# A routed mixture-of-experts kernel: one lookup of slots moved behind the first turned slots, the row copies issued from GpSimd, two counts put into one PSUM bank

## The chip, the cores and the metric

The kernel runs on one core of a Trainium2 chip. A core has a matrix engine (TensorE, "PE" in the profile, with its weight loads "PEld"), a vector engine (VectorE, "DVE"), a scalar engine (ScalarE, "ACT"), GpSimd ("POOL") and SyncE ("SP"), each with its own in-order instruction queue. They share an on-chip memory of 128 partitions (SBUF) and a small accumulator memory (PSUM) in eight banks, which TensorE writes and DVE and ACT read. DMA transfers are issued from the queues of SP, ACT and GpSimd. The metric is the device time of one execution in microseconds (us).

## The reference, cut to what matters

```python
xn  = layernorm(x)                                   # 8192 tokens of 512
out = x + attn(xn) + ffn(xn)

def attn(x):                                         # random features
    feats   = AB/sqrt(512) * exp(x @ (ab*G).T - 0.5*|x|^2*ab^2)
    return feats @ weights.T                         # weights: the same map of a 512x512 matrix

def ffn(x):                                          # 64 experts, 8 per token, at most 256 slots each
    scores = sigmoid(x @ router_w)
    # keep the 4 best of 8 groups of experts, then the 8 best experts
    w      = topk / sum(topk) * 2.5
    pos    = how many earlier (token, choice) pairs went to the same expert
    # the first 256 tokens of each expert fill its slots
    y[e]   = (silu(slots[e] @ gate[e]) * (slots[e] @ up[e])) @ down[e]
    return scatter_add(y * w) + shared_expert(x)
```

## The kernel before

Every product that must be exact is made from a high and a low part (`products`: three matmuls of high·high, high·low and low·high for each 128-row piece); `upper` (ACT, line 98) makes the high part and `rest` (DVE, line 101) the low one.

**Routing stage.** The 8192 tokens are 16 blocks of 512. `dense(b)` runs for the even blocks only and yields ten times: two steps of the shared expert (`ps_gu`), four of the random features (`ps_f`), four of the outputs (`ps_o`, first the shared expert's down product, then the attention). After each step `routing` moves the front of up to two blocks on, so that one pair of blocks passes in ten steps. A block's front is the generator `look_up`: it turns the block's rows (`ps_x`, line 331), forms the logits (`ps_l`, 364), turns them back (`ps_lt`, 381), ranks groups and experts on DVE (397 to 438), and two steps later counts: `ps_b` (443) gives for each expert the tokens in earlier chunks, `ps_u` (454) the running count within chunks, which ACT copies to `cu` (462) and SP stores to DRAM as `upto`. In the step after that DVE adds `ps_b` up in `begun` (482, two rows). By then the next block's front has started. In the first five steps of a pair (ps_gu, ps_f) the counts belong to an even block and the turning to an odd one; in the last five (ps_f, ps_o) the other way round.

**The rows of a block.** `statistics` (275, 278) and `roots` (DVE 241, 242, then thirteen small steps on GpSimd, 246 to 290, and four more for the norms to 294) feed `normalize`, in which ACT writes the normed rows to `xw` (301), two tiles of two 128-row groups. From block 5 on, `xc` (314) is a plain DMA copy of `xw`, 512 KB a tile, that TensorE may read as float32r, in which it turns the rows faster; it is issued from ACT's queue.

**PSUM.** Three pools: `ps_tr` (two banks), `ps_mm` (four), `ps_sm` (two, tag "sm"). `ps_l`, `ps_lt`, `ps_b`, `ps_u`, half of the `ps_x` tiles, and later `ps_fu` and `ps_y` of the late blocks' attention take the two "sm" banks in turn. A tile gets a bank once its last user has read it.

**Hand-over to the experts.** `seek` (the generator `slots`) finds which token fills which slot. Each step issues two lookups `at` from GpSimd (`find`, 699); once four experts are there, `tokens_of` (711 to 720) counts on DVE and gives `who`, the indices of the gathers `xg` (752, GpSimd). Eight steps run at the end of the last dense block, then gathers for experts 0 to 3. Then the last four steps of a late block's attention (`ps_y`; DVE copies each to `yb`, 594) take two more steps of `slots`, the second of which holds `tokens_of` for experts 4 to 7. Its DVE rows are kept behind what `last["dve"]` names. `turn_slots(0)` turns the first expert's gathered rows (`ps_t`, 769), splits them into `gT`, and computes their weights `shares` and `we` (779, 783).

**Experts' stage.** For each expert: `hidden` (`ps_gu` in 256 columns), `turn_slots` of the next, pieces of the late blocks' attention, `down` (`ps_e`), and a scatter-add of the rows from GpSimd (819). Weights come by SP.

**Order.** A scheduler fixes each engine's order when the program is built. `behind(a, b)` forces a behind b without a wait; `in_turn` keeps GpSimd's lookups, gathers and scatters in program order. Waits are semaphores that the framework places.

Of the kernel before, what the change touches and what calls it, by code (L numbers as in the profile page):

```python
# [9 lines left out]
FP = mybir.dt.float32  # L10
# [8 lines left out]
P = 128  # L19
T = 8192  # L20
H = 512
R = 512
E = 64
# [8 lines left out]
TB = 512  # L32
NB = T // TB
NS = TB // P
# [19 lines left out]
def rfs_attention_moe_kernel(  # L54
# [15 lines left out]
    nc = tc.nc  # L70
# [6 lines left out]
    ps_sm = ctx.enter_context(tc.tile_pool(name="ps_sm", bufs=2, space=PSUM))  # L77
# [6 lines left out]
    def kib4(shape, name, dt=FPR):  # L84
        return four.tile(shape, dt, tag="four", name=name)
# [11 lines left out]
    def upper(dst, src):  # L97
        return nc.scalar.copy(dst, src)  # L98

    def rest(dst, src, hi, on=nc.vector):  # L100
        return on.tensor_tensor(dst, src, hi.bitcast(FP), ALU.subtract)  # L101
# [15 lines left out]
    def behind(a, b):  # L117

        tc.add_manual_dep(a.ins, b.ins.name, ORDER, reason="what a needs comes late")
# [38 lines left out]
    def store_rows(b, k, xb):  # L158

        r0 = b * TB + k * UT  # L160
        return nc.sync.dma_start(
            out[r0 : r0 + UT, :].rearrange("(s p) d -> p s d", p=P), xb.t[k]
        )

    last = {}
# [131 lines left out]
    def normalize(b, rstd, shift):  # L297
        xb = xbs[b]
        xw = [rows.tile([P, NH, XW], FP, tag="xw", name="xw") for _ in range(NS // NH)]
        for s in range(NS):  # L300
            normed_s = nc.scalar.activation(
                xw[s // NH][:, s % NH, :H],
                xb[s],
                AF.Identity,
                bias=shift[:, s : s + 1],
                scale=rstd[:, s : s + 1],
            )
            behind(normed_s, last["upper"])
        xc = None
        if b >= ROUND:  # L310

            xc = [kib4([P, NH, H], "xc", FP) for _ in xw]
            for t, w in zip(xc, xw):
                nc.scalar.dma_start(t, w[:, :, :H])
        if b % 2:

            for k in range(TB // UT):
                store_rows(b, k, xb)
            del xbs[b]
        return xw, xc  # L320
# [22 lines left out]
    def look_up(b):  # L343
# [90 lines left out]
        for s in range(1, NS):  # L434
# [4 lines left out]
        yield  # L439
        yield  # L440

        pb = ps_sm.tile([P, NS, E], FP, tag="sm", name="ps_b")
        counted = nc.tensor.matmul(
            pb.rearrange("p s e -> p (s e)"),
            ones_r,
            prior_r.rearrange("p s e -> p (s e)"),
            start=True,
            stop=True,
        )
        behind(counted, last["pe"])  # L450
        pu = ps_sm.tile([P, NS // 2, P], FP, tag="sm", name="ps_u")
        for q in range(NS // 2):
            for part, (w, v) in enumerate(((mask_r, tri_r), (prior_r, ones_r))):
                nc.tensor.matmul(
# [172 lines left out]
    rest(rwp[:, :, 1, :], rw_sb, rwp[:, :, 0, :], nc.gpsimd)  # L627
    normed = {}
    normed[0] = normalize(0, *roots(0, statistics(xbs[0], NS * [last["rest"]]), nc.vector))
    first = last["shift"]  # L630
    roots1 = roots(1, statistics(xbs[1], NS * [first]))
# [12 lines left out]
    def split_gates(gu):  # L644
        return list(zip(*(split(t, "gu") for t in gu)))
# [6 lines left out]
    for rc in range(RC):  # L652
        pool, tag = ((ps_sm, "sm"), (ps_tr, "tr"))[rc // 2]
        ps_w.append(pool.tile([P, H], FP, tag=tag, name="ps_f"))
        projected(parts(wT, KC), rc, ps_w[rc])
    late = look_up(0)
    next(late)
    upper0 = last["upper"]
    sup = split(sgu[1], "gu", (upper0, last["rest"]))
    fw = Chunks(RC, "fw", FP)  # L660
    for rc in range(RC):
        exponents = exponent(fw[rc], wn, rc, ps_w[rc])
        behind(exponents, last["rest"])
    normed[1] = normalize(1, *roots1)
    eab = const.tile([P, RC], FP, name="eab")
    behind(nc.scalar.activation(eab, ab, AF.Exp), upper0)
# [55 lines left out]
    def seek():  # L722

        chunks()
        ats = {}
        for e in range(E + TE):
            n, k = divmod(e, TE)
            if e < E:
                if k == 0:
                    ats[n] = kib4([P, TE, NH, P], "at", FP)  # L730
                find(ats[n], e)
            if k == 1 and n:
                tokens_of(n - 1, ats.pop(n - 1), last["dve"])
            yield
# [25 lines left out]
    def turn_slots(e):  # L760
        xg = xgs.pop(e)
        xr = xg.bitcast(FPR)
        gp = [kib4([P, KC, CAP], "gT") for _ in range(2)]
        for c2 in range(KC // 2):
            pr = ps_tr.tile([P, 2, CAP], FPR, tag="tr", name="ps_t")
            ps = pr.bitcast(FP)
            for c in range(2):
                for h in range(NH):
                    turned_s = nc.tensor.transpose(  # L769
                        pr[:, c, ts(h, P)], xr[:, h, ts(c2 * 2 + c, P)], ident_r  # L770
                    )
                    if e == 0:
                        behind(turned_s, last["pe"])
            cs = slice(2 * c2, 2 * c2 + 2)
            upper(gp[0][:, cs, :], ps)
            turned_r = rest(gp[1][:, cs, :], ps, gp[0][:, cs, :])

        we = rt.tile([P, NH], FP, tag="we", name="we", bufs=4)
        shares = nc.vector.scalar_tensor_tensor(
            we, xg[:, :, H + e], 1.0, xg[:, :, H + E], ALU.add, ALU.mult  # L780
        )
        behind(shares, turned_r)
        nc.vector.reciprocal(we, we)
        wes[e] = we
        return gp

    def hidden(e, gp, w):
# [46 lines left out]
    slots = seek()  # L834
# [6 lines left out]
    def routing(t):  # L841

        for b in sorted(fronts):
            if next(fronts[b], fronts) is fronts:
                del fronts[b]
        b, k = divmod(t + GAP, GAP)
        if k == (b == 1) and b < NB:
            fronts[b] = look_up(b)
            next(fronts[b])
        if k == GAP - 3 and b + 1 < NB:  # L850
            normed[b + 1] = normalize(b + 1, *roots(b + 1, statistics(xbs[b + 1])))
        if k == 1 and b + 2 < NB:
            xbs[b + 2] = load_tokens(b + 2)
# [22 lines left out]

    for n in range(NS):
        next(rest_of)
        if n < 2:
            next(slots)  # L880
        if n == 0:
            gws[0] = split_gates(gates.pop(0))
    rest_steps -= RC + NS
    gps[0] = turn_slots(0)
    yes = [kib4([P, NH, H], "ye", FP) for _ in range(3)]

    def ends():
# [38 lines left out]
    for i in range(E + 1):  # L926


        if i + 2 < E:
            gates[i + 2] = load_gates(i + 2)  # L930
        if i + 1 < E:
            downs[i + 1] = load_down(i + 1)
        if i < E:
            hps[i] = hidden(i, gps.pop(i), gws.pop(i))
        next(slots, None)
        if i + 4 < E:
            gather(i + 4)
        if i + 1 < E:
            gps[i + 1] = turn_slots(i + 1)
            gws[i + 1] = split_gates(gates.pop(i + 1))  # L940
        for _ in range(rest_steps * i // E, rest_steps * (i + 1) // E):
            next(rest_of, None)
        if i >= E - 2:
            next(last_of)
        if i == E:

            next(last_of)
        if i > 0:
            down(i - 1, hps.pop(i - 1), dws.pop(i - 1))
        if i < E:  # L950
            dws[i] = split_down(downs.pop(i))
            if i == E - 2:

                last["down"] = last["split"]
# [40 lines left out]
```

## Time and profile before

| | |
|---|---|
| time, median of 3 runs | 1320.38 us (1320.17 to 1323.96) |
| profiled execution | 1324.84 us, its span 1323.1 us |
| granted TensorE clock, mean | 0.998 |
| DMA, mean | 256 GB/s, 338.60 MB |
| xc from ACT's queue | 22 issues, 512 KB each |
| lookups and gathers from GpSimd | 128 and 128, median landing 6.4 and 7.1 us after issue |

The span is the profiled execution between its first and last instruction. A row of the timeline is start, duration, engine, line, operation, output and inputs; "x4" merges four instructions, and a bracket gives the idle time just before and what ended it. "ACTq" and "SPq" are the queues' sequencers issuing DMAs. Matmuls overlap, so their durations are longer than the distance from one start to the next. The engine order of instructions, which the scheduler makes of each version, is known without a run and carries no times.

### The profile page before, as it was taken

The page shows a single profiled execution, that of the slowest core. Times are in us where ns is not written, and L with a number is a line of the kernel's source. Part 1 is how long each engine was busy: PE and PEld are TensorE (multiplying, and loading weights), DVE is VectorE, ACT ScalarE, POOL GpSimd, SP SyncE. Part 2 cuts the span into 40 slices and gives each one's busy share as a digit, 9 for nine tenths or more (in the row PEclk, how much of TensorE's full clock was granted, in tenths as well). Part 3 has the DMA queues.
Part 4 walks back from the last instruction along what each step waited for, and adds up shares of the span by engine and source line. Part 5 has one row for each costly group of instructions (what it writes and reads, how often), then busy time and mean ns, then how long its engine had stood idle before and what let it go on. Part 6 is the DMA issues. An engine that isn't in the chain of part 4 may idle for free.

```text
span 1323.1 us, 21351 instructions
## 1 busy us (share of the span) xinstructions
PE 1300.0 (98%) x7648; PEld 1138.6 (86%) x7648; DVE 929.2 (70%) x1922; ACT 646.1 (49%) x1017; POOL 573.1 (43%) x670
## 2 busy tenths in 40 slices
PE   8999999999999999999999999999999999999998
PEld 6888787788788899999999999999999999988886
DVE  7978768768765677777677767777776776643555
ACT  5644443444332455656556556655565565540111
POOL 3122012012105667778667676767677754210000
PEclk9999999999999999999999999999999999999999
DMA  7665675675585989999999999999999999875995
GB/s 253 239 229 198 234 259 197 233 266 209 193 314 178 305 216 306 270 276 271 317 271 264 309 265 283 248 294 285 266 259 303 281 259 234 227 220 178 317 319 191
DMA packets 192313, 338.60 MB, mean 256 GB/s; under 512 B 15952, under 2 KB 87632, under 8 KB 192208
## 3 DMA queue, kind: packets, MB, share of 16 engines
q1 hardware_dynamic: 153456, 245.93, 54.1%
q0 software_dynamic: 32768, 79.78, 27.3%
q10 hardware_dynamic: 5984, 11.54, 2.5%
q8 instruction: 60, 0.98, 0.3%
q14 instruction: 45, 0.37, 0.1%
HBM read 220.66 MB, written 104.99 MB: 246 GB/s over the span
## 4 chain that ended last, share of the span: by engine, by line
PE 90%; DVE 4%; DMA 4%; ACT 1%; issue 1%; POOL 0%; SPq 0%; DVEq 0%; ACTq 0%
PE ps_gu L108 41%; PE ps_o L108 14%; PE ps_e L108 13%; PE ps_fu L108 6%; PE ps_y L108 5%; PE ps_f L108 3%; PE ps_t L769 3%; DMA xc<-xw 2%; PE ps_l L364 2%; PE ps_x L331 2%; DMA xb<-in_L_attn_x_dram 1%; DVE f L491 0%; DVE r L499 0%; DVE fT L101 0%; DVE st L275 0%
## 5 line engine op out<-in xcount | busy, mean ns | idle before, releaser
L819 POOL DMA_INDIRECT out_dram<-ye,who x128 | 225.5, 1762 | 186.5 <-ACT ye L818 136.4
L108 PE MATMUL ps_gu<-gT,gu_h 128*128 128x256 f32 x2048 | 291.3, 284 | 0.0
L108 PEld LDWEIGHTS ps_gu<-gT,gu_h 128*128 128x128 f32 x2048 | 268.6, 192 | 5.3 <-ACT gu_h L98 1.0
L699 POOL DMA_INDIRECT at<-upto,line x128 | 140.2, 1095 | 80.1 <-DMA q<-norms 41.4
L108 PE MATMUL ps_gu<-gT,gu_l 128*128 128x256 f32 x1024 | 167.3, 286 | 0.2 <-DVE gu_l L101 0.2
L101 DVE TENSOR_TENSOR gu_l<-gu,gu_h 128x1024 fp32r<-128x1024 f32 x128 | 155.6, 1218 | 6.9 <-ACT gu_h L98 6.9
L752 POOL DMA_INDIRECT xg<-xnw,who x128 | 143.1, 1118 | 39.0 <-issue 32.6
L108 PE MATMUL ps_e<-d_h,ehT 128*128 128x512 f32 x512 | 148.6, 392 | 0.0
L108 PEld LDWEIGHTS ps_gu<-gT,gu_l 128*128 128x128 f32 x1024 | 140.9, 192 | 0.7 <-DVE gu_l L101 0.4
L98 ACT CAST gu_h<-gu 128x1024 fp32r<-128x1024 f32 x128 | 132.5, 1058 | 0.0
L246 POOL TENSOR_TENSOR a<-rstd,ve 128x4 f32<-128x4 f32 x45 | 10.5, 233 | 272.0 <-DVE rstd L242 269.6
L98 ACT CAST ehT<-sg 128x512 fp32r<-128x512 f32 x64 | 39.8, 621 | 156.6 <-DVE sg L499 153.7
L818 ACT ACTIVATE ye<-ps_e,we 128x512 f32<-128x512 f32 x128 | 88.6, 695 | 56.4 <-PE ps_e L108 55.6
L108 PEld LDWEIGHTS ps_e<-d_h,ehT 128*128 128x128 f32 x512 | 94.7, 188 | 18.8
L499 DVE SCALAR_TENSOR_TENSOR sg<-sg,ps_gu 128x512 f32<-128x512 f32 x64 | 44.0, 688 | 68.4 <-PE ps_gu L108 68.2
L101 DVE TENSOR_TENSOR d_l<-d,d_h 128x1024 fp32r<-128x1024 f32 x64 | 78.3, 1224 | 7.6 <-ACT d_h L98 7.2
L101 DVE TENSOR_TENSOR gT<-ps_t,gT 128x512 fp32r<-128x512 f32 x128 | 83.2, 682 | 0.0
L101 DVE TENSOR_TENSOR ehT<-sg,ehT 128x512 fp32r<-128x512 f32 x64 | 44.4, 694 | 51.8 <-ACT ehT L98 51.8
L505 ACT ACTIVATE f<-f,ab 128x512 f32<-128x512 f32 x64 | 46.4, 725 | 69.3 <-DVE f L491 69.3
L108 PE MATMUL ps_o<-fW_h,fT 128*128 128x512 f32 x288 | 79.3, 392 | 0.2 <-ACT fT L98 0.2
L108 PE MATMUL ps_e<-d_l,ehT 128*128 128x512 f32 x256 | 79.4, 391 | 0.0
L108 PE MATMUL ps_o<-d_h,hT 128*128 128x512 f32 x256 | 78.3, 396 | 0.0
(180 smaller groups left out, 2513.6 us busy)
## 6 DMA issues: line engine op xcount, KB each, us to landing
gu<-in_L_ffn_gate_w_dram SPq DMA_DIRECT2D x64, 512.0 KB
gu<-in_L_ffn_up_w_dram SPq DMA_DIRECT2D x64, 512.0 KB
d<-in_L_ffn_down_w_dram SPq DMA_DIRECT2D x64, 512.0 KB
xnw<-xw SPq DMA_DIRECT2D x32, 577.0 KB
xb<-in_L_attn_x_dram SPq DMA_DIRECT2D x32, 512.0 KB
out_dram<-xb SPq DMA_DIRECT2D x32, 512.0 KB
xT_h<-turned SPq DMA_DIRECT2D x30, 512.0 KB
xT_l<-turned SPq DMA_DIRECT2D x30, 512.0 KB
```

The source lines that it names most:

```text
L98: return nc.scalar.copy(dst, src)
L101: return on.tensor_tensor(dst, src, hi.bitcast(FP), ALU.subtract)
L108: last["pe"] = nc.tensor.matmul(ps, w[c][a], v[c][b], start=(start and part == 0 and c == 0), stop=(stop and part == 2 and c == n - 1),)
L331: last["turn"] = nc.tensor.transpose(pr[:, ts(s, P)], src(s)[:, ts(kc, P)], ident if dt is FP else ident_r)
L364: logits = nc.tensor.matmul(pl, rwp[:, kc].rearrange("p t e -> p (t e)"), v[kc], start=(n == 0 and kc == 0), stop=(n == 1 and kc == KC - 1),)
L499: nc.vector.scalar_tensor_tensor(dst, dst, 0.5, u, ALU.mult, ALU.mult)
L505: nc.scalar.activation(f, f, AF.Exp, scale=ab[:, rc : rc + 1])
L699: nc.gpsimd.indirect_dma_start(out=at[:, e % TE, h, :], out_offset=None, in_=upto, in_offset=bass.IndirectOffsetOnAxis(ap=line[:, e, h : h ...
L752: nc.gpsimd.indirect_dma_start(out=xgs[e][:, h, :], out_offset=None, in_=xnw, in_offset=bass.IndirectOffsetOnAxis(ap=who[:, e, h : h + 1], ...
L769: turned_s = nc.tensor.transpose(pr[:, c, ts(h, P)], xr[:, h, ts(c2 * 2 + c, P)], ident_r)
L818: nc.scalar.activation(ye[:, h, :], po, AF.Copy, scale=wes[e][:, h : h + 1])
L819: now = nc.gpsimd.indirect_dma_start(out=out, out_offset=bass.IndirectOffsetOnAxis(ap=who[:, e, h : h + 1], axis=0), in_=ye[:, h, :], in_o ...
```

## The change

Three things change:

- the counts `ps_b` and `ps_u` become two halves of one "sm" tile, so of one PSUM bank;
- `xc` is issued from GpSimd's queue;
- before the experts, only one of the two steps of `slots` runs inside the late attention's last steps; the other one stands behind `turn_slots(0)`, and `shares` of the first expert becomes what its DVE rows stay behind.

```diff
@@ normalize
             for t, w in zip(xc, xw):
-                nc.scalar.dma_start(t, w[:, :, :H])
+                nc.gpsimd.dma_start(t, w[:, :, :H])
@@ look_up
-        pb = ps_sm.tile([P, NS, E], FP, tag="sm", name="ps_b")
+
+        both = ps_sm.tile([P, 2, TB // 2], FP, tag="sm", name="ps_bu")
+        pb = both[:, 0].rearrange("p (s e) -> p s e", e=E)
         counted = nc.tensor.matmul(
-            pb.rearrange("p s e -> p (s e)"),
+            both[:, 0],
...
-        pu = ps_sm.tile([P, NS // 2, P], FP, tag="sm", name="ps_u")
+        pu = both[:, 1].rearrange("p (q t) -> p q t", t=P)
@@ turn_slots
         wes[e] = we
+        if e == 0:
+
+            last["dve"] = shares
         return gp
@@ the hand-over
     for n in range(NS):
         next(rest_of)
-        if n < 2:
+        if n == 0:
             next(slots)
-        if n == 0:
             gws[0] = split_gates(gates.pop(0))
     rest_steps -= RC + NS
     gps[0] = turn_slots(0)
+    next(slots)
```

In the order of instructions that the scheduler makes of the new version, `ps_l` stands right behind the counts (before: three or four other matmuls between). In the second half of a pair the counts stand three matmuls of `ps_o` earlier. On DVE the rows of `tokens_of` for experts 4 to 7 come behind `we` of the first expert, and some statistics and `begun` rows change places. GpSimd's order changes only by the 22 copies; in odd blocks from 7 to 13 the second copy stands behind the first three steps of the next block's root. SP's order changes by places of single stores. `begun` gets a wait for ACT's copy `cu` of the same bank.

## The prediction

> **What bounds it now.** I read the page's busy line first, then the table of stretches, TensorE's waits, and the chain's lines in time. The page and the stretches (columns: stretch, its length, then busy us of PE, its weight loads, DVE, ACT and POOL, granted clock, DMA share, GB/s):
>
> ```profile
> PE 1300.0 (98%) x7648; PEld 1138.6 (86%) x7648; DVE 929.2 (70%) x1922; ACT 646.1 (49%) x1017; POOL 573.1 (43%) x670
> ...
> 33.00:425.00 392.00, 383.93 (x1878) 316.28 (x1878) 296.60 (x944) 172.37 (x326) 68.40 (x253) 1.00 0.64 229
> 425.00:460.00 35.00, 31.90 (x195) 28.48 (x194) 19.89 (x33) 10.25 (x16) 23.35 (x22) 0.95 0.98 313
> 460.00:1160.00 700.00, 699.81 (x4760) 643.39 (x4759) 505.58 (x759) 416.04 (x603) 463.75 (x344) 1.00 0.97 270
> ```
>
> TensorE is the bound; its idle time is the most that can be won. The experts' stage (460 to 1160) has none and starts whenever the routing stage is done, so what is won before 460 comes out at the end. The routing stage idles 8 us by the busy column, the hand-over to the experts 3. TensorE's waits (us in all, times, longest):
>
> ```profile
> PE ps_x L331 <- DMA xc<-xw: 5.0, 5, 1.5
> PE ps_fu L108 <- DVE yb L594: 2.8, 1, 2.8
> PE ps_l L364 <- ACT cu L462: 1.5, 7, 0.2
> PE ps_l L364 <- DVE xw L471: 1.2, 5, 0.2
> ```
>
> Each of the change's three parts stands on one of these rows. Busy time hides some loss, because the modelled end of a matmul overlaps its successor. So I measure start to start: four 512-column matmuls take 0.907 us here. One pair of blocks, TensorE alone:
>
> ```profile
> 283.79 1.14 PE L108 MATMUL ps_f<-xT_h,pT_h 128*128 128x512 f32 x4
> 285.14 1.21 PE L364 MATMUL ps_l<-xT_h,rwp 128*128 128x512 f32 x4 [0.22 <-ACT cu L462]
> 286.19 1.08 PE L364 MATMUL ps_l<-xT_l,rwp 128*128 128x512 f32 x4
> ...
> 297.56 0.28 PE L331 MATMUL ps_x<-ident_r,xc 128*128 128x128 f32 x2
> 298.63 1.39 PE L331 MATMUL ps_x<-ident_r,xc 128*128 128x128 f32 x14 [0.78 <-DMA xc<-xw]
> ```
>
> **A. Two counts in one bank.** Today ps_b and ps_u take both "sm" banks. The logits ps_l need one back: ps_u's after ACT's copy cu, or ps_b's after DVE's second begun. In the rows, 283.79 to 285.14 is 1.35 for 0.91, a loss of 0.44, and the next four lose 0.14 more. Over the stage: seven such places at 0.58, all in the first half of a pair (ps_gu, ps_f), and five in the second (ps_o) at 0.47, together 6.4 us. With one bank for both, ps_l takes the other, which the turned blocks left long before; in the new order of instructions ps_l stands right behind the counts. Changing tile costs some hundredths each time. I take **-6.0**, bounds -6.4 and -3.
>
> [...] Today cu (307.24 to 307.61) and begun (306.85 to 307.81) overlap; now begun must stand behind cu, and the built program does make begun wait for cu. [...] By the rows 15 are covered: in the first halves hT (0.69) is now put ahead of begun, and DVE then idles 3.5 before f; in the second about 2.0 us of DVE rows (L546, L467, L275, small ones) stand ahead of it, and cu ends some 1.3 after the last L435. Behind begun are the next statistics and, in the bank, ps_lt, both over a microsecond later. Only block 15 pays: begun, line, first lookup, first gather and first turned slots are one chain: **+0.4**.
>
> **B. GpSimd issues the copies xc.** It removes 22 issues of 0.60 from ACT's queue; ACT is 44% busy here, so that alone is nothing. What counts is when a copy starts. In even blocks (6 to 14) ACT finishes xw at 283.2 but reaches its xc issues only at 290.68 and 292.40, behind f, fT and lt. The copy lands 6.1 to 7.0 us after the second issue, and the 14 transposes wait: 1.00, 1.62, 0.81, 0.90 and 1.30 beyond the pace, 5.6 us. GpSimd has nothing else queued then, so the copy starts at 283 and lands near 291, needed at 297.6: five microseconds of cover.
>
> Not all 5.6 arrive. DVE runs without a gap from 291.3 to 306.3, and the counts ps_b (loads at 306.30) need its last L435 (305.52 + 0.21 = 305.73). The new order takes three matmuls (0.68) from ahead of ps_b and one 0.69 row from ahead of that L435. So ps_b can come 0.57 + 0.61 - 0.68 = 0.5 us earlier, and the rest of the 0.9 becomes a wait for DVE. Five times 0.5: **-2.5**, bounds -5.6 (if DVE moves along) and 0.
>
> Odd blocks (7 to 15) are the danger. Their copy is issued just in time and read 6.35 us later without a wait:
>
> ```profile
> 318.74 0.60 ACTq L314 DMA_DIRECT2D xc<-xw  x1
> ...
> 325.09 1.15 PE L331 MATMUL ps_x<-ident_r,xc 128*128 128x128 f32 x12
> ```
>
> On GpSimd's in-order queue the second copy stands behind the first and three steps of the next block's root (0.28 each). No row shows a plain copy from GpSimd. The nearest are its gathers: an issue takes 0.94 at least, 2.03 at most; landing:
>
> ```profile
> DMA to landing us min/median/max: 3.6/7.1/9.2
> ```
>
> [...] DVE's statistics reach their last root step (L242) about 1.8 us earlier: begun's 0.53 wait is covered, L546 and one 0.66 row of statistics move behind. So xw is ready at 316.9 instead of 318.7, and the second copy starts at 317.3 to 318.2, landing at 323.9 to 325.7. TensorE comes about 1.0 earlier (0.5 from ps_b, 0.5 from ps_l), to the third transpose at 324.15. A wait of 0 to 1.5; I take 0.4 for each of five, **+2.0**, bounds 0 and +7.5. Even blocks' roots are now behind these copies: 271.4 becomes about 275, and ACT uses them at 279.8.
>
> **C. The second lookup.** At the hand-over, DVE:
>
> ```profile
> 433.34 1.23 DVE L711 TENSOR_TENSOR at<-at,slot 128x1024 f32<-128x1024 f32 x1 [3.40 <-DMA xg<-xnw,who]
> 434.48 2.35 DVE L101 TENSOR_TENSOR gu_l<-gu,gu_h 128x1024 fp32r<-128x1024 f32 x2
> 436.75 1.21 DVE L716 TENSOR_REDUCE tok<-at 128x8 f32<-128x1024 f32 x1
> 437.88 0.68 DVE L594 COPY yb<-ps_y 128x512 f32<-128x512 f32 x1
> ...
> 438.55 0.69 DVE L594 COPY yb<-ps_y 128x512 f32<-128x512 f32 x1
> 438.61 0.73 PE L108 MATMUL ps_fu<-xT_h,pT_h 128*128 128x512 f32 x2 [2.75 <-DVE yb L594]
> ```
>
> L711 stands 3.4 us at the head of DVE's queue, waiting for rows; behind it are the splits gu_l and the copies yb that free the bank for ps_fu. Moved behind shares, it lets gu_l start at 430 and the yb copies run as ps_y ends (432.3 and 434.5), so ps_fu follows the turned slots at 435.9: 2.75 won. The low halves gT_l come at 436.2 instead of 439.22; the ten ps_gu behind ps_fu now run 1.0 us over their pace waiting for them, of which I keep 0.7. **-3.4**, bounds -4 and -1.5. Late next is the gather xg, whose 0.34 stays. The moved step issues lookups too: SP's queue does not change, and GpSimd's keeps its order, since each lookup still follows its predecessor. The moved rows (L711 to L720, 2.9 us) then run at about 438 to 441; who is needed by the fifth expert's gather at 446.7 and DVE's next row at about 441.5. If that cover goes, up to 1 us returns.
>
> **Sum.** -6.0 + 0.4 - 2.5 + 2.0 - 3.4 = -9.5. The profiled execution took 1324.84 (span 1323.1), so it would take 1315.3. The median of the runs is 1320.38, 4.5 below the profiled one; the waits are of the program, not of that slower run, so the forecast is 1320.4 - 9.5, about **1311**.
>
> **Rivals.**
> - *DVE becomes the bound of the second halves* (chance 0.20). For it: 15 us without a gap. Against: DVE idles 3.5 elsewhere in each pair. Then B gives nothing and A's five second-half places give nothing (2.3 back): -9.5 + 2.5 + 2.3, about 1316.
> - *The copies land late in odd blocks and set the stage* (0.15), slower. With the longest issue row (2.03) and the landing at 9.5 from the second issue at 318.2, the wait is 318.2 + 9.5 - 324.15 = 3.55, five times 17.7 in place of 2.0: -9.5 + 15.7 = +6.2, 1326.6. It decides from an odd wait of 2.3 us on (11.5 over five). For it: the latest gathers. Against: those are from a stage with a DMA share of 0.97; here it is 0.64.
> - *The copy moves nothing, odd waits eat what even ones give, and C finds the gather late* (0.10): about A alone with half of C, -6 + 0.4 - 1.7, 1313.
> - The forecast: 0.55.
>
> The range holds all but the slow rival and the ends: low from A -6.4, B -5.6, C -4 and no odd wait, 1305; high at 1319, past the DVE rival. 0.3% is 4 us, about what a measurement of this kernel can tell from no change: faster (below 1316.4) has 0.70, same 0.14 (half of the DVE rival falls there), slower 0.16.
>
> **What would show it.** ps_l without a wait, and begun waiting for cu only where TensorE does not: A. No xc wait in even blocks, a small one in odd, with ps_b waiting for L435: B. ps_fu without its 2.75 and L711 at about 438: C. An odd xc wait over 2.3 us, GpSimd copy issues over 2 us, or ps_lt waiting for begun would prove me wrong.

## The result, and the profile after

| | before | changed |
|---|---|---|
| time, median | 1320.28 us (6 runs, 1319.47 to 1323.96) | 1310.63 us (6 runs, 1310.21 to 1311.31) |
| profiled execution, its span | 1324.84, 1323.1 us | 1310.94, 1309.2 us |
| first to last `ps_lt` (blocks 0 to 15) | 354.37 us | 345.19 us |
| last `ps_lt` to first `ps_t` | 47.80 us | 47.81 us |
| first `ps_t` to first `ps_e` | 21.98 us | 16.86 us |
| first `ps_e` to the end | 866.6 us | 866.4 us |

The ratio of the times is 0.9921, 95% interval 0.9907 to 0.9935: 10.4 us of 1320.3, with 8.6 and 12.3 as the ends. The lower rows are starts in the two profiled timelines. What moved lies in two places, the routing stage (9.2 us) and the hand-over to the experts (5.1 us), and together they are 14 us, 4 more than the medians differ by. That gap is the main question below.

The same stretches as before (stretch, its length, busy us of PE, its weight loads, DVE, ACT, POOL, clock, DMA share, GB/s), in the changed kernel:

```profile
33.00:425.00 392.00, 390.59 (x1920) 324.26 (x1921) 296.33 (x949) 171.87 (x326) 91.80 (x282) 1.00 0.66 235
425.00:460.00 35.00, 35.00 (x251) 32.35 (x250) 26.98 (x43) 20.42 (x30) 25.14 (x23) 1.00 1.01 316
460.00:1160.00 700.00, 700.00 (x4728) 642.17 (x4728) 502.03 (x753) 412.19 (x598) 450.47 (x339) 1.00 0.97 272
```

TensorE idles 1.4 us in the first stretch, where it was 8, and not at all in the second, whose clock went from 0.95 to 1.00. POOL is 23 us busier in the first, 17 of it the 22 issues of the copies. All waits of TensorE that the view lists (us in all, times, longest):

```profile
PE ps_x L331 <- DMA wi<-_attn_input_weights_dram: 5.1, 3, 3.7
PE ps_bu L445 <- DVE prior_r L435: 0.9, 3, 0.3
PE ps_lt L381 <- ACT lt L374: 0.6, 2, 0.4
PE ps_o L108 <- ACT fT L98: 0.2, 1, 0.2
```

The four rows of before that the prediction shows are gone: `ps_x` for `xc`, `ps_fu` for `yb`, and both of `ps_l`. One is new that the change brings, the counts' wait for DVE's last prior sum. In TensorE's timeline it stands in the second half of a pair:

```profile
292.22 1.49 PE L331 MATMUL ps_x<-ident_r,xc 128*128 128x128 f32 x16
...
299.21 0.61 PE L108 MATMUL ps_o<-fW_h,fT 128*128 128x512 f32 x2
300.16 0.36 PE L445 MATMUL ps_bu<-prior_r,ones_r 128*128 128x256 f32 x1 [0.34 <-DVE prior_r L435]
...
300.75 1.15 PE L364 MATMUL ps_l<-xT_h,rwp 128*128 128x512 f32 x4
```

The sixteen transposes run as one group, and `ps_l` starts right behind the counts. Of the copies, the view of the tile `xc` says (duration of an issue, then issue to landing):

```profile
L314 POOL DMA_DIRECT2D xc<-xw x22: 722/769/982, 122.9 to 358.6; - x22
...
DMA to landing us min/median/max: 3.2/5.0/6.8
```

And `begun`, which now shares its bank with `cu`, in the view of its line: 32 rows of the same length as before (476 ns), and a single wait, in block 15:

```profile
L484 DVE SCALAR_TENSOR_TENSOR begun<-ps_bu,slot,begun x32: 471/476/485, 56.7 to 394.2; 128x256 f32<-128x256 f32 x32
its engine sat idle before it (us, times) until:
  ACT cu L464: 0.2, 1
```

### The profile page after: what moved, and what is told of

The parts are those of the page before. It is cut to its first block, busy times and chain, and to the rows that moved or that the text cites. A ratio compares the mean times of both kernels' runs of the same rounds, so it can differ in the third digit from the quotient of the medians.

```text
span 1309.2 us, 21368 instructions
## 1 busy us (share of the span) xinstructions
PE 1296.7 (99%) x7648; PEld 1138.6 (87%) x7648; DVE 925.0 (71%) x1922; ACT 645.2 (49%) x1017; POOL 581.7 (44%) x692
## 4 chain that ended last, share of the span: by engine, by line
PE 91%; DVE 4%; DMA 2%; SPq 1%; ACT 1%; issue 1%; POOL 0%; DVEq 0%; ACTq 0%
PE ps_gu L108 41%; PE ps_e L108 13%; PE ps_o L108 13%; PE ps_y L108 6%; PE ps_fu L108 6%; PE ps_f L108 4%; PE ps_t L771 3%; PE ps_x L331 2%; PE ps_l L364 2%; DMA xb<-in_L_attn_x_dram 1%; DVE st L275 1%; DMA xT_l<-turned 1%; SPq L262 1%; DVE xT_l L101 1%; DMA gu<-in_L_ffn_up_w_dram 0%
## 5 line engine op out<-in xcount | busy, mean ns | idle before, releaser
L754 POOL DMA_INDIRECT xg<-xnw,who x128 | 137.3, 1073 | 39.0 <-issue 32.0
```

The lines of the kernel that those rows point to most:

```text
L754: nc.gpsimd.indirect_dma_start(out=xgs[e][:, h, :], out_offset=None, in_=xnw, in_offset=bass.IndirectOffsetOnAxis(ap=who[:, e, h : h + 1], ...
```

## The experiments

### Each part alone, and the stall filled

A alone (e1) puts both counts into one tile, B alone (e2) is the one word that names the queue, C alone (e3) moves the lookup. The fourth kernel (e4) is the kernel before with work for TensorE in the stall, and with `behind` ties that put this work between `ps_t` and `ps_fu`. Of each edit the main lines:

```diff
 e1  +        both = ps_sm.tile([P, 2, TB // 2], FP, tag="sm", name="ps_bu")
     ...
 e2  -                nc.scalar.dma_start(t, w[:, :, :H])
     +                nc.gpsimd.dma_start(t, w[:, :, :H])
 e3  -        if n < 2:
     +        if n == 0:
             next(slots)
     ...
     +    next(slots)
 e4  +    fill = ps_mm.tile([P, TB], FP, tag="mm", name="ps_fill")
     +    for i in range(11):
     +        filled = nc.tensor.matmul(
     +            fill, fW[0][i % RC][:, :P], fW[0][i % RC], start=i == 0, stop=i == 10
     +        )
     ...
```

> Part A alone: the two counts share one bank, the copies stay on ACT's queue and both lookups stay ahead of the experts. The forecast's term is -6.0 + 0.4 = -5.6 us, so about 1314.7 against 1320.3 (bounds -2.6 to -6.0). The theory that A's place in the second halves is worth nothing (DVE bounds them) expects about -3.3, 1317. Read from the two profiles of before and after, A is about -5. In its profile ps_l should have no wait, the ps_x waits for xc (5 us) and the 2.75 us wait of ps_fu should still be there, and begun should wait for cu only where DVE is ahead of TensorE.

> Part B alone: the 22 copies on GpSimd's queue. The forecast's term is -2.5 + 2.0 = -0.5 us, so about 1319.8; bounds -5.6 to +7.5. The changed kernel's trace suggests something else: no xc wait in even blocks and none in odd ones, issues of 0.77 instead of 1.0 to 2.0, and a new wait of the counts for DVE's last prior sum of 0.34 each, some 1.8 in all: then B is about -4, 1316. If the gain seen there was A's and not B's, B alone is within 1 us of before.

> Part C alone: the second lookup behind the first expert's turned slots. The forecast's term is -3.4 us, so 1316.9 (bounds -1.5 to -4). The two traces show 3.5 won up to ps_fu and 1.6 more up to the first ps_e, with the granted clock at 0.93 and 0.73 in the ten microseconds around the stall before and at 1.00 after. If the clock's drop comes with the stall in every execution, C is about -5.0, 1315.3, and the clock is 1.00 at the hand-over. If the drop was one execution's chance, C is -3.4 to -3.5.

> The kernel before, with eleven extra matmuls of 512 columns (11 x 0.227 = 2.5 us), whose result nothing uses, put between the turned slots of the first expert and ps_fu, where TensorE waits 2.75 us for the copy yb. The wait itself stays: the bank of ps_fu is still freed late. Theory 1, an idle TensorE makes its clock drop for some microseconds after: the granted clock at the hand-over is 1.00 and the kernel is 1 to 2 us faster than before, although it does more work. Theory 2, the slow matmuls behind ps_fu wait for the low halves gT_l and the clock's row is a coincidence: the same time as before or up to 0.3 us more.

Measured, beside 38 runs of the kernel before (median 1321.79):

| | median, us | ratio to before | interval |
|---|---|---|---|
| A alone | 1315.10 | 0.9951 | 0.9933 to 0.9969 |
| B alone | 1317.24 | 0.9958 | 0.9942 to 0.9974 |
| C alone | 1319.74 | 0.9984 | 0.9976 to 0.9992 |
| stall filled | 1322.73 | 1.0004 | 0.9994 to 1.0014 |

That is -6.5, -5.6 and -2.1 us: 14.2 in all, again about 4 more than the three give together. Where A and B overlap is seen in the starts. For each place between 120 and 388 us, this is how far the next group starts later than the matmuls before it need (0.227 us for one of 512 columns, 0.085 for a transpose of `ps_x`), summed:

| us lost | before | A alone | B alone | all three |
|---|---|---|---|---|
| `ps_x` for `xc`, five even blocks | 5.6 | 4.7 | 0 | 0 |
| ahead of `ps_l`, six first halves | 2.7 | 0.3 | 2.7 | 0.3 |
| ahead of `ps_l`, five second halves | 2.4 | 0.3 | 0.0 | 0.3 |
| ahead of the counts, second halves | 0.0 | 0.0 | 0.2 | 1.6 |
| sum, less than before | | 5.4 | 7.8 | 8.5 |
| first to last `ps_lt`, less than before | | 6.5 | 7.8 | 9.2 |

The second halves' `ps_l` are won by either part. With B alone the counts stand three matmuls of `ps_o` earlier, so that the banks are free again when `ps_l` comes, though there are still two tiles. The forecast had this order before it and booked its gain under A only.

C is another matter. B alone and A alone have the same order of instructions at the hand-over as the kernel before. DVE's second lookup in B alone, then in A alone:

```profile
425.92 1.23 DVE L711 TENSOR_TENSOR at<-at,slot 128x1024 f32<-128x1024 f32 x1 [3.43 <-DMA xg<-xnw,who]
```

```profile
425.41 1.22 DVE L713 TENSOR_TENSOR at<-at,slot 128x1024 f32<-128x1024 f32 x1 [1.08 <-DMA xg<-xnw,who]
```

The wait has two sizes. With the long one (3.40 in the first profile of before, 3.43 here) `ps_fu` waits 2.75 and 3.3 us; with the short one it waits 1.00.

The traces show what goes with the size. The view names the gathers `xg`, but this row reads `at`, and it starts 0.1 to 0.3 us behind the landing of the last of the sixteen lookups that GpSimd issues ahead of the gathers. In the three profiles with a long wait (before, e2 and e4) the thirteenth lookup takes 1.57 to 1.61 us to issue, in the other eleven 0.94 or 0.95. In before, then in A alone, with the DVE row that starts with it:

```profile
421.37 1.61 POOL L699 DMA_INDIRECT at<-upto,line  x1 [0.30 <-issue]
421.43 0.69 DVE L101 TENSOR_TENSOR fU<-f,fU 128x512 fp32r<-128x512 f32 x1
```

```profile
415.75 0.94 POOL L701 DMA_INDIRECT at<-upto,line  x1 [0.30 <-issue]
415.87 0.68 DVE L101 TENSOR_TENSOR fU<-f,fU 128x512 fp32r<-128x512 f32 x1
```

In the three, DVE's row starts 0.06 or 0.07 us behind the start of this issue; where it starts 0.12 us behind it (e1, e3, e11, e12) the issue has its usual length, and in the other seven no such row starts during it. After the long issue the sixteenth lookup is issued 39.3 to 39.5 us behind the last `ps_lt` instead of 38.0 to 38.7, and lands 7 us after its issue (6.9 to 7.3) instead of 3.3 to 5.9. So a shift of some 0.05 us between two engines goes with 2.3 us of waiting. The two go together in all fourteen profiles; whether the one brings about the other was not shown.

The long wait has a second price. TensorE's granted clock, a microsecond at a time (the column after the five engines), in the kernel before and in B alone:

```profile
439.00:440.00 1.00, 1.00 (x7) 0.96 (x6) 1.00 (x5) 0.00 (x0) 0.80 (x1) 0.65 0.82 291
440.00:441.00 1.00, 1.00 (x7) 1.00 (x7) 0.82 (x3) 0.00 (x0) 0.70 (x2) 0.50 0.88 232
441.00:442.00 1.00, 1.00 (x8) 1.00 (x7) 0.00 (x0) 0.00 (x0) 0.69 (x2) 0.50 0.97 377
442.00:443.00 1.00, 1.00 (x8) 1.00 (x7) 0.00 (x0) 0.00 (x0) 0.70 (x2) 0.64 1.03 362
443.00:444.00 1.00, 1.00 (x11) 1.00 (x10) 0.00 (x0) 0.00 (x0) 0.90 (x1) 1.00 1.12 377
```

```profile
431.00:432.00 1.00, 0.81 (x2) 0.71 (x3) 1.00 (x5) 0.00 (x0) 0.69 (x2) 0.68 0.82 301
432.00:433.00 1.00, 1.00 (x6) 0.91 (x6) 1.00 (x3) 0.00 (x0) 0.74 (x1) 0.50 0.98 208
433.00:434.00 1.00, 1.00 (x6) 1.00 (x6) 0.40 (x3) 0.00 (x0) 0.94 (x1) 0.50 0.71 242
434.00:435.00 1.00, 1.00 (x9) 1.00 (x8) 0.00 (x0) 0.00 (x0) 0.71 (x1) 0.61 1.01 374
```

Right behind the stall the clock falls to half for 3.4 us: TensorE is busy all the time and gets 6 to 8 matmuls done in a microsecond instead of 11. The missing shares add up to 0.35 + 0.50 + 0.50 + 0.36 = 1.7 us in each of the two. In A alone, after a wait of 1.00, the clock stays at 1.00. From the first `ps_t` to the first `ps_e` it takes 21.98 us in before and 22.02 with B alone, 18.14 with A alone, and 16.83 with C alone. So C is worth 5.1 us where the wait is long and 1.3 where it is short (18.14 against 16.83, both without a long wait).

How often is it long? Of the 38 runs of before that stand beside these four kernels, 11 have a mean granted clock of 0.998 or less (median 1324.85), the other 27 have 0.999 or 1.000 (median 1321.06). With C alone it is 1 of 22 (1324.11; the others' median 1319.66, 1.4 below that of the 27), and with the whole change none of 11. That the runs with the lower clock are those with the long wait is inferred: runs without a profile show no waits, and one half-clock stretch is only 1.7 of 1320 us, so that a mean of 0.999 can hide it. The two values for C, weighted with 11 and 27 runs, give an estimate of 2.4; measured were 2.1.

The filled stall (e4) tells what made the clock fall. TensorE's rows and clock there, with the lookup's wait long again (3.20):

```profile
434.97 2.76 PE L895 MATMUL ps_fill<-fW_h 128*128 128x512 f32 x11
438.22 0.73 PE L109 MATMUL ps_fu<-xT_h,pT_h 128*128 128x512 f32 x2 [0.49 <-DVE yb L599]
```

```profile
439.00:440.00 1.00, 0.85 (x6) 0.51 (x4) 1.00 (x3) 0.00 (x0) 0.76 (x1) 1.00 1.01 195
440.00:441.00 1.00, 0.82 (x7) 0.76 (x7) 0.43 (x3) 0.00 (x0) 0.93 (x1) 1.00 0.69 246
```

`ps_fu` starts as late as before, with no useful work done meanwhile; TensorE idles 0.49 us ahead of it instead of 2.75, and the clock stays at 1.00 in this profile. The mean is 0.999 or more in all 14 runs. So the fall to 0.50 went with the idle time here, not with the stage or its data, as theory 1 has it. (e12, below, adds a case from the routing stage.) Its forecast of 1 to 2 us less fails (median +0.9; by the ratio +0.5, between -0.8 and +1.9). In the profile the way from `ps_t` to `ps_e` is 20.81 us, 1.2 less than before. But where the wait is only 1.0, 2.5 us of filler would delay `ps_fu` by 1.5: an estimate with 27 runs of 38 at +1.5 and 11 at -1.2 gives +0.7.

### Two parts at a time

```diff
 e5  A and C:  nc.scalar.dma_start(t, w[:, :, :H])      # xc as before
 e6  B and C:  pb, pu in two tiles of tag "sm"          # counts as before
 e7  A and B:  if n < 2: next(slots)                    # both lookups as before
 e8  the kernel before, unchanged
```

> Parts A and C, the copies xc back on ACT's queue. Alone, A gave -6.5 us, B -5.6 and C -2.1, 14.2 together, but the three together gave 9.7 to 10.4. Theory 1, A and B overlap by some 4 us (both remove the wait of the second halves' ps_l for xw, and the xc waits that A leaves take up part of what A wins): -8, about 1312.5 to 1313, so B's share of the whole change is about 2. Theory 2, the parts add up and the single ones were measured too large: about -4.5, B's share 5 to 6. Its profile should keep four to five waits of ps_x for xc, 3 to 5 us in all.

> Parts B and C, the two counts in two banks again. Theory 1, overlap: -7 to -8, about 1313.5, so A's share of the whole change is 2.5 to 3.5; in the profile the first halves' ps_l <- cu (1.5 us by busy time, 3 to 4 by starts) is there, and the second halves' ps_l <- xw is not, because B has moved the counts three matmuls of ps_o forward. Theory 2, sizes add up: -4 to -5.

> Parts A and B, both lookups ahead of the experts as before. Theory 1, the wait of the second lookup has two sizes from one execution to the next (1.08 us with one bank alone, 3.40 before, 3.43 with the copies alone) and only the long one makes the clock drop: most executions at about 1312, 1 to 2 us above the whole change, with a mean clock of 0.999 or 1.000, and some 4 us more at 0.996 to 0.998; never all alike. Theory 2, the stall is the same each time and C's worth is 3.4 to 5: all at 1314 to 1315.5.

> The kernel before once more, for a second profile. Theory 1: if its time is about 1321, the second lookup's wait is about 1.1 us, ps_fu waits about 1, and the granted clock at the hand-over is 1.00; if its time is about 1325, the rows are those of the first profile (3.4, 2.75, 0.73). Theory 2, the stall is the same each time: 3.4 and 2.75 at either time.

Times, beside a median of 1334.48 (62 runs) for the kernel before on this chip: e5 1330.02 (0.9964, 0.9948 to 0.9980), e6 1334.27 (0.9992, 0.9983 to 1.0001), e7 1327.19 (0.9959, 0.9935 to 0.9982), e8 1334.78 (1.0004, 0.9988 to 1.0021). The times here say nothing of the parts: all four profiles, that of the kernel before too, lose 5 to 21 us between the last `ps_lt` and the first `ps_t`, in which every other profile but one takes 47.8 (e9 48.6). DVE in e6, then TensorE in e6, then TensorE in e8:

```profile
438.21 0.69 DVE L546 TENSOR_TENSOR xb<-ps_o,xb 128x512 f32<-128x512 f32 x1 [18.90 <-remote]
```

```profile
441.21 2.08 PE L108 MATMUL ps_y<-fW_h,fU 128*128 128x512 f32 x4 [14.52 <-DVE yb L594]
```

```profile
426.10 0.79 PE L108 MATMUL ps_y<-fW_h,fU 128*128 128x512 f32 x1 [3.58 <-ACT fU L98]
```

DVE stands still for 18.9 us, and TensorE waits for the copy behind it. What DVE waited for cannot be read: from the first lookups on these four traces lack semaphore events (some 15,500 in each, 19,000 in the others), they know the landing of no transfer, and "remote" only says that no releaser was found. On the chip of e1 to e4 there is nothing of it. The cause stays open, and with it what e7 and e8 were to show of the lookup's wait (e7's times do lie in two groups, 1325 to 1328 and 1335, which fits either story). What is not touched is the routing stage ahead of it. From the first to the last `ps_lt`, in all profiles:

| | us in each profile | mean | less than neither |
|---|---|---|---|
| neither A nor B (before, e3, e4, e8) | 354.4, 353.0, 353.5, 352.8 | 353.4 | |
| A (e1, e5) | 347.9, 349.1 | 348.5 | 4.9 |
| B (e2, e6) | 346.5, 346.7 | 346.6 | 6.8 |
| A and B (after, e7, e9) | 345.2, 344.7, 344.7 | 344.9 | 8.5 |

Theory 1 holds: the parts overlap by 4.9 + 6.8 - 8.5 = 3.2 us. With B in place A is worth 1.7, with A in place B is worth 3.6. Profiles of one row differ by up to 1.6 us, so these are good to about 1 us. The first profile of before, at 354.4, is the longest of its four here too.

This answers the question of the 4 us. The profile of before was long in both places, by about 1 us in the routing stage and by 3.8 at the hand-over. With 8.5 for A and B and 2.1 for C the whole is 10.6, where the medians and the ratio say 9.7 to 10.4.

### What B leaves behind

```diff
 e10  +            if hold is not None and kc == KC - 1:
      +                behind(last["rest"], hold)            # hold: the last prior sum
 e11  -                nc.gpsimd.dma_start(t, w[:, :, :H])
      +                nc.sync.dma_start(t, w[:, :, :H])
 e12  -        for b in sorted(fronts):
      +        for b in sorted(fronts, reverse=True):
 ...
```

> The changed kernel once more, beside the kernel before on this chip, as the base for the next three. Theory: the gain does not depend on the chip where the hand-over to the experts runs undisturbed: -9.5 to -10.5 us. From the first to the last turned logits (ps_lt of block 0 to block 15) it takes 345.2 us as in its first profile, within 0.5.

> The changed kernel with one pair of DVE rows exchanged in each even block from 6 on: the last prior sum goes ahead of the block's last low half xT_l. Theory 1, what B could not bring in is a matter of DVE's order: the waits of ps_bu for prior_r (0.34 each, 1.8 in all by starts) go, and the stage from the first to the last ps_lt takes 343.5 to 344.2 instead of 345.2; 1.0 to 1.7 us faster than the changed kernel. Theory 2, DVE bounds the second halves: the wait comes back as ps_l for the later xT_l, and the stage and the time stay within 0.3.

> The changed kernel with the copies xc issued from SP's queue; TensorE's and DVE's order stays. Theory 1, what counts is only that the copy starts as soon as xw is written, not which queue issues it, and descriptors written by GpSimd wait for nothing here: the same time as the changed kernel within 0.5 us, if SP's queue is free when xw is ready. Theory 2, SP's in-order queue holds the copies behind stores that still wait: waits of ps_x for xc come back, up to 5 us in all. [...]

> The changed kernel with the front of the newer block moved on ahead of the older one's in each step: the counts come behind ps_l and ps_lt. Theory 1: the wait for prior_r goes as in the exchange of the two rows, 1.0 to 1.7 us. Theory 2: ps_l now comes before its low halves xT_l are ready and waits, and the next front's DVE rows push the prior sums back, so nothing is gained or up to 3 us lost.

| beside before at 1321.46 (11 runs) | median, us | ratio | interval | first to last `ps_lt` | ahead of the counts |
|---|---|---|---|---|---|
| e9, the change again | 1311.21 | 0.9919 | 0.9903 to 0.9935 | 344.7 | 1.5 |
| e10, prior sum first | 1310.07 | 0.9912 | 0.9893 to 0.9931 | 344.3 | 1.1 |
| e11, copies from SP | 1308.84 | 0.9906 | 0.9887 to 0.9925 | 343.0 | 0.1 |
| e12, newer front first | 1313.21 | 0.9937 | 0.9921 to 0.9952 | 347.0 | 0.0 |

The change repeats itself on a third chip. The exchange of two DVE rows (e10) is 1.1 us better by the medians, but its interval overlaps that of the changed kernel almost wholly and the stage is only 0.4 shorter, so this is not clear of noise; the loss ahead of the counts goes from 1.5 to 1.1, a part of what theory 1 said. Into the place that it freed, ahead of the last prior sum, the order that was built puts another row, the 0.68 us of `xb`'s addition; the counts start 0.36 us behind the start of that sum, as in the changed kernel (298.61 and 298.97 here, 299.80 and 300.16 there). The copies from SP (e11) beat the changed kernel by 2.4 us, three of their four runs below its fastest one; the intervals of the ratios overlap, so the size is not settled. Neither theory said that. DVE's and TensorE's orders are the same in both, and no `ps_x` waits for `xc` in either; the counts' wait is what went. DVE's timeline in the changed kernel shows where it came from:

```profile
286.60 0.42 DVE L389 TENSOR_TENSOR lt<-ps_lt,lt 128x256 f32<-128x256 f32 x1
287.52 0.69 DVE L275 BATCH_NORM_STATS2 st<-xb 128x6 f32<-128x512 f32 x1 [0.50 <-DMA xb<-in_L_attn_x_dram]
```

From there DVE runs without a gap to the last prior sum, so the 0.50 us of waiting for the next tokens `xb` is still there at 300. Place by place the two go together: in the two profiles of the changed kernel (after, e9) L275 waits in six of the ten pairs from block 5 on, and these six lose 0.31 to 0.50 us ahead of the counts, the other four at most 0.22. In e11, as in before, no row of L275 waits for `xb` (nor in e10, whose 1.1 us are lost in another order of DVE's rows). SP's queue, in the changed kernel and in e11 (the block's transposes come at 292.22 and at 290.25):

```profile
280.74 2.61 SPq L262 DMA_DIRECT2D norms<-sq  x4
283.39 0.92 SPq L149 DMA_DIRECT2D xb<-in_L_attn_x_dram  x2
```

```profile
278.77 1.33 SPq L262 DMA_DIRECT2D norms<-sq  x4
280.14 0.91 SPq L149 DMA_DIRECT2D xb<-in_L_attn_x_dram  x2
281.15 1.30 SPq L314 DMA_DIRECT2D xc<-xw  x2
```

With GpSimd's two copies under way (issued at 276.77 and 278.66) the four small stores of the norms hold SP's queue for 2.61 us, and the load of `xb` behind them is issued 8.8 us ahead of the transposes; with the copies behind it in SP's own queue they take 1.33, and it is 10.1 ahead. Whether the copies in flight make the difference of 1.28 was not tried by itself.

The newer front first (e12) gains the counts' wait and loses more elsewhere. Once it shows what the slow rival was about, a copy that TensorE waits for until 8 us after its issue (at 124.37). Its clock two microseconds later:

```profile
132.44 1.98 PE L331 MATMUL ps_x<-ident_r,xc 128*128 128x128 f32 x14 [3.05 <-DMA xc<-xw]
```

```profile
134.00:135.00 1.00, 1.00 (x6) 0.90 (x5) 1.00 (x3) 1.00 (x4) 0.00 (x0) 0.50 0.14 57
```

Here too the half clock follows the stall, far from the hand-over: the fourteen transposes take 1.77 us from start to start and the four matmuls behind them 1.79, where 1.19 and 0.91 are the pace. Three of e12's six runs have a mean clock of 0.998 or less although C is in place, so a low mean has more than one cause.

## Why the prediction was right, and where it was not

1311 was forecast and 1310.63 measured. Each part won where it was said to, but that the total came out so close is luck: A and B together gave 2.4 us more than forecast and C 1.3 less, and the two errors nearly cancel.

- **A, one bank.** Forecast -6.0, measured -4.9 alone and -1.7 beside B. `ps_l` has no wait any more, as said. The places were sized a fifth too high; that five of the twelve, 2.4 us, would be won by B as well was overlooked. The +0.4 for block 15 did not come: from `ps_b` to `begun` it takes 1.12 us instead of 0.81, but the first lookup is issued 3.96 us behind `ps_b` (3.98 before), and the first `ps_t` starts 47.8 us behind the last `ps_lt` in both. The wait of `begun` for `cu` shows once in 32 rows, with 0.2 us; the other 15 blocks show none, as forecast.
- **B, even blocks.** Forecast -2.5. All 5.6 of the `xc` waits went and 1.6 came back as the counts' wait for L435, so -4.0. The place of the new wait was right, its size not: the forecast had 3.1 kept. Most of the 1.6 goes with the wait for `xb`, which the forecast did not have; where no row waits for `xb` and none was exchanged, DVE's chain kept 0.2 (B alone) and 0.1 (e11).
- **B, odd blocks.** Forecast +2.0, measured 0. The copy issued at 312.99 is read at 319.01 without a wait. The term stood on an issue of 1.0 to 1.9 and 6.6 to 7.5 to land, an estimate of the author's from the nearest rows, the gathers, and no run shows it for a copy of the odd blocks: a plain copy of 512 KB takes 0.72 to 0.98 to issue and 5.0 to land at the median, and in the odd blocks 7 to 13 only 3.2 to 3.9. The longest of the 22 issues is 0.26 us above the shortest. Against the other queues the runs show only the issue, 0.77 us at the median here, 0.60 from ACT in before and 0.61 from SP in e11: no landing of a copy from ACT or SP is in the traces. With gathers of scattered rows as neighbours, "nearest" was not near.
- **A and B together**: forecast -6.1, measured -8.5.
- **C, the second lookup.** Forecast -3.4, measured -1.3 in the common case, -5.1 in the profiled one, -2.1 over the runs. The order behind the change is as said: L713 at 428.29 (2.4 us behind `ps_t`), `ps_fu` right behind the turned slots, 0.62 us after their start. The step that failed is the sentence "the waits are of the program, not of that slower run". The profiled execution was 4.5 us above the median, and 3.8 of it are this wait with the half clock behind it. L711 did not wait for rows that are always late but for lookups that were late in this execution. The gathers behind them were late with them: the 0.34 us of `ps_t` for `xg`, which the forecast kept, is gone in the changed kernel and in A alone. Also the 1.0 us by which the ten `ps_gu` ran over their pace was no wait for gT_l: it is gone in A alone (twelve in 1.42 us, 2.44 before), where gT_l comes as late behind `ps_fu` as before and the clock stays whole. The half clock stood behind 2.75 us of waiting in the profile of before, and there was none behind 1.00 in that of A alone. The clock's column, 0.95 at the hand-over in the prediction's own table of stretches, pointed to it.

The rivals: DVE does hold back the second halves, but by 1.6 us and not by the 4.8 of that case. The late copies did not come: no odd wait reached 2.3 us in the changed kernel. Nor did the third rival's case, for the even waits are gone and nothing came in odd blocks. For the profiled execution 1315.3 was forecast, and the changed kernel's took 1310.94: there the errors show, 4.4 us; between the medians they cancel.

## What to carry to other kernels

When the profiled execution is slower than the median, first ask which of its waits made it so: a wait for a DMA may be the difference itself (here 3.8 of 4.5 us, with the clock behind it), and then its removal is worth less in the median than the row says (2.1 us where the profiles gave 5.1). A second profile of the same order tells. Price a stall of TensorE by the clock behind it as well as by its length (here 1.7 us behind 2.75), and read the clock a microsecond at a time there. Where two parts of a change touch one order of instructions, list each place once, and ask of each part alone whether it already frees it.

## What the runs showed of the hardware

- After 2.75 (before) and 3.3 us (e2) without a matmul, TensorE's granted clock went to 0.50 for 3.4 us (1.7 us lost), and after 3.05 us (e12) it was 0.50 from 134 to 135 us; after 1.0 us (e1) and 1.5 us (before, at `xc`), or with unused matmuls in the gap (e4), it stayed at 1.00.
- The same instruction, in the same order, waited 1.08 us for a landing in one profile and 3.40, 3.43 and 3.20 in three others. With the long wait one lookup's issue on GpSimd took 1.57 to 1.61 us instead of 0.94, each time when DVE's row of `fU` (0.69 us) started 0.06 or 0.07 us behind it, and not when it started 0.12 us behind it.
- A plain 512 KB copy issued by GpSimd took 0.77 us of its queue (0.61 from SP) and landed after 5.0 us at the median, sooner than its gathers (7.1).
- On the chip of e5 to e8 all four kernels lost 5 to 21 us in the 48 us before the hand-over, with DVE standing still for up to 18.9 us; their traces lack part of the events, and the cause is open.
